# Turning an attention mask with 32x32 squares on the vector engine, in place of transposing DMAs

## The chip, the core and the metric

The kernel runs on one core of one Trainium2 chip. A core has a matrix engine (PE, with a weight-load track PEld), a vector engine (DVE), an activation engine (ACT), a general engine (POOL), and a queue engine (SP) that here only issues DMAs. The engines run their own instruction streams in order and wait for one another by semaphores. The time is device microseconds (us) of one execution.

## The reference, cut to what matters

Two graph-attention layers run over 16 batches of 1024 tokens with 256 features. `x` is float32, `adj` is an int32 matrix of zeros and ones, one per batch, and the same `adj` masks both layers.

```
for layer in (0, 1):                      # 4 heads of 64, then 8 heads of 32
    h = relu(layernorm(x))
    q, k, v = h @ Wq, h @ Wk, h @ Wv      # per head
    s = q @ k.T / sqrt(D)                 # 1024 x 1024 per head and batch
    s = where(adj > 0, s, -inf)           # row: the token that asks; column: the key
    x = x + softmax(s) @ v @ Wo + bo
```

## The kernel before, in words

**Tiling.** Everything is float32 except the mask. The scores are computed transposed: a PE matmul (L450) leaves 128 keys on the partitions and 512 asking tokens (a "half", `qh`) along the row, in a PSUM pair `ps` of 2 x 512. The DVE (L473, `exponentials`) combines a pair with the mask and writes it to SBUF as `p`; ACT (L479) takes the exponential in place; PE (L491, `weigh`) multiplies by the values into `po`. The sums of the exponentials come from POOL, which adds `p` tiles (L604), from accumulating DMAs `p<-p` (L588), and from a matmul with ones (`pz`, L343). They travel through `spread` (`sums`), `invert` (L383, then a DMA to `vd`) and `fetch` (DMAs to `inv`), and POOL scales the output `cat` with them (L402). `end_half` multiplies by Wo (L432) and adds to `x` (L437).

**Steps.** The work is a list of steps written out by hand. A step is a tile of scores: in layer 0 two key tiles of two heads, in layer 1 one key tile of four heads. The list runs layer 0 of batch 0, then for each batch `b` the 16 steps of layer 0 of batch `b+1` and the 32 steps of layer 1 of batch `b`. In the lists of due times `a` is the index of the first of these layer-0 steps, `c = a + 16` that of the first layer-1 step. I write c+7 for the layer-1 step with that index. PE issues the scores of a step two steps (LEAD) ahead of its `weigh`. There are three `ps` pairs, and every other PSUM product (`pq`, `pv`, `py`, `ph`) takes one of the same three. Layer-0 steps are run two at a time.

**Other work** (`Stream.later`) is hung on steps by number. Within a step or pair of steps the dues run after the step's own exponentials, in order of their step, and the PE-heavy ones (turn, k, q, values, end_half) run last of all. The order on every engine is thus fixed by these numbers. Layer-0 exponentials of two steps are added up by `add_tiles`: the DVE does L500 and L503, POOL the rest (L503 to L506).

**The mask** (`class Mask`, eight tiles of 128 asking tokens per batch) takes three steps. `load` (L148): a POOL DMA reads 128 rows of `adj`, 1024 int32 each, and casts to bf16. `flip` (L154): a transposing DMA from SP turns the 128 x 1024 tile so that the keys lie on the partitions. `put` (L163): ACT writes it as fp8 numbers of plus or minus 8192 into `mask[128, 8 key tiles, 512 tokens]`. The DVE reads 512 neighbouring fp8 numbers of one key tile in L473. For layer 1 `second` (L171) turns the same marks into 0 and 16384 in place. The pool `adjp` holds one `adj` and one `adjT` tile.

**Order of tokens.** `quarters` places `x` so that partition 32g+p, tile t, holds token 512 half + 128 g + 32 t + p.

**Statistics.** `norms(inp, half, i1, i2, i3, i4)` hangs the layer norm on four steps: statistics of tiles 0 and 1 on i1, of tiles 2 and 3 on i2 with the last small DVE operations (L195, L197) and POOL's power (L199, L201), then ACT's normalisation (L210) of tiles 0, 1 on i3 and of tiles 2, 3 on i4. For batch 0 layer 1 and for the first inputs `turn` then transposes on PE (L232); for the others `turn_blocks` transposes 32x32 squares on the DVE (L236) and DMAs put the squares in place (`turned`, `hT`).

Of the kernel before, what the change touches and what calls it, by code (L numbers as in the profile page):

```python
# [88 lines left out]
def fast_program(ctx, tc, a, w, loads, chk):  # L89
# [7 lines left out]
    QH = N // 512  # L97

    xp = ctx.enter_context(tc.tile_pool(name="xp", bufs=3))
    adjp = ctx.enter_context(tc.tile_pool(name="adjp", bufs=1))  # L100
    actp = ctx.enter_context(tc.tile_pool(name="actp", bufs=2))
    work = ctx.enter_context(tc.tile_pool(name="work", bufs=2))
    pp = ctx.enter_context(tc.tile_pool(name="pp", bufs=2))
# [14 lines left out]

    def quarters(of, b, half):

        rows = of[b, ts(half, 512), :].rearrange("(g t p) e -> g p t e", g=4, p=32)
        return [rows[g] for g in range(4)]

    def by_tile(cols):
# [13 lines left out]

    class Mask:
        def __init__(self, b):  # L140
            self.b, self.src, self.flipped, self.m = b, {}, {}, {}

        def load(self, t, at=None):

            if at is None:
                at = adjp.tile([P, N], BF16, tag="adj", name=f"adj_{self.b}_{t}")
            self.src[t] = at
            nc.gpsimd.dma_start(at, adj[self.b, ts(t, P), :])  # L148

        def flip(self, t, to=None):  # L150
            if to is None:
                to = adjp.tile([P, NT, P], BF16, tag="adjT", name=f"adjT_{self.b}_{t}")
            self.flipped[t] = to
            nc.sync.dma_start_transpose(to, self.src.pop(t))  # L154

        def put(self, t):

            qh = t // 4
            if t % 4 == 0:
                self.m[qh] = actp.tile(  # L160
                    [P, NT, 512], F8, tag="mask", bufs=5, name=f"mask_{self.b}_{qh}"
                )
            nc.scalar.activation(  # L163
                self.m[qh][:, :, ts(t % 4, P)], self.flipped.pop(t), AF.Identity,
                bias=w.below, scale=2.0 * EDGE, saturate=False,
            )

        def second(self, u):

            m = self.m[u // 4][:, ts(u % 4, 2), :]  # L170
            nc.scalar.activation(m, m, AF.Abs, bias=w.above, saturate=False)  # L171


# [138 lines left out]
    class Group:  # L312
# [46 lines left out]
        def spread(self):  # L359

            s = work.tile([P, 512], F32, tag="inv", name=f"s_{self.n}")
            nc.scalar.copy(tiled(s), by_tile(self.s))
            inp, k = self.inp, 2 * self.qh + self.g if self.layer else self.qh
            if k == 0:

                pool, tag = small, f"sums{self.layer}"
                if self.layer and inp.b == B - 1:
                    pool, tag = adjp, "adj"
                inp.sums = pool.tile(
                    [P, (4 if self.layer else 2) * self.n_f], F32, tag=tag, bufs=1,  # L370
                    name=f"sums_{inp.n}",
                )
            self.sn = inp.sums[:, ts(k, self.n_f)]
            for r in range(4):
                nc.sync.dma_start(
                    self.sn[ts(r, 32), :],
                    s[32 * r : 32 * r + 1, :].rearrange("r (c f) -> r c f", f=self.n_f),
                )
# [78 lines left out]
    def exponentials(st, between):  # L457


        gr = st.gr  # L460
        odd = st.j % 2
        if odd:
            st.p = None
            st.halves = [
                pp.tile([P, 2, 512], F32, tag=f"p1{i}", bufs=2, name=f"p_{st.n}_{i}") for i in range(2)
            ]
        else:
            st.p = pp.tile([P, 4, 512], F32, tag="p0", bufs=7, name=f"p_{st.n}")
            st.halves = [st.p[:, ts(i, 2), :] for i in range(2)]
        for i in range(2):  # L470
            half = st.halves[i]
            kt = st.blocks[2 * i][1]
            nc.vector.scalar_tensor_tensor(  # L473
                out=half,
                in0=gr.mask.m[gr.qh][:, kt, :].unsqueeze(1).to_broadcast([P, 2, 512]),
                scalar=-EDGE if gr.layer else BIG, in1=st.ps[i],
                op0=ALU.add if gr.layer else ALU.mult, op1=ALU.min,
            )
            nc.scalar.activation(half, half, AF.Exp, scale=gr.scale)  # L479
            if i == 0:  # L480
                for f in between:
                    f()
# [34 lines left out]
    class Stream:  # L517
# [12 lines left out]
        def later(self, i, f, *args):  # L530
            self.due.setdefault(i, []).append((f, args))
# [132 lines left out]
    def open_w(n):  # L664
# [7 lines left out]
    open_x(0, 0)  # L672


    stage = [pp.tile([P, 4, N], BF16, tag="p0", bufs=7, name=f"adj_0{i}") for i in range(2)]
    stage_t = [
        pp.tile([P, 2, NT, P], BF16, tag=f"p1{i}", bufs=2, name=f"adjT_0{i}") for i in range(2)
    ]

    def load(u):  # L680
        masks[0].load(u, stage[u // 4][:, u % 4, :])

    open_w(3)
    open_x(0, 1)
# [6 lines left out]
    load(3)  # L691
    inp.turn(0)

    def flip(u):
        to = stage[0][:, u % 4, :].rearrange("p (t q) -> p t q", q=P)
        masks[0].flip(u, stage_t[u // 2][:, u % 2, :, :] if u < 4 else to)

    flip(0)
    flip(1)
    open_w(1)  # L700
    inp.k(0)
    inp.norm(1, whole=True)
# [1 line left out]
        load(u)  # L704
    inp.q(0)
    inp.turn(1)
    mask.put(0)
    mask.put(1)
    inp.values(0)
    flip(2)  # L710
    open_x(1, 0)
    flip(3)
    open_w(5)
    open_x(1, 1)
    inp.k(1)
    mask.put(2)
    mask.put(3)
    inp.q(1)
    inp.values(1)
    open_w(len(loads))  # L720
# [29 lines left out]
    def norms(inp, half, *at, whole=False, bias=None):  # L750

        for i, f in zip(at, (inp.stats, inp.stats, inp.norm, inp.norm)):
            rest = (whole,) if i in at[2:] else ()
            later(i, f, half, (0, 1) if i in (at[0], at[2]) else (2, 3), *rest)
        later(at[3] + 1 if bias is None else bias, inp.add_bias, half)
# [13 lines left out]


    for u in range(4, NT):
        later((u - 4) // 2, flip, u)
        later(u - 1, mask.put, u)
    for t in range(NT):
        i = 5 + 2 * t
        later(i - 3, masks[1].load, t)
        later(i - 2, masks[1].flip, t)
        later(i, masks[1].put, t)
    later(9, bias_of_v)
    norms(inputs[0][1], 0, 2, 3, 5, 6, whole=True)  # L780
    half_inputs(inputs[0][1], 0, 7, 8, 10, 12)
# [2 lines left out]
    for b in range(B - 1):  # L784
        mine, a, c = inputs[1][b], first[b + 1], second[b]
        if b == 0:

            norms(mine, 0, a + 5, a + 6, a + 8, a + 9, whole=True)
            half_inputs(mine, 0, a + 11, a + 12, a + 14, a + 14)
            norms(mine, 1, a + 13, a + 14, a + 15, c, whole=True)  # L790
            half_inputs(mine, 1, c + 1, c + 3, c + 6, c + 4)
        else:
            norms(mine, 0, a - 20, a - 16, a - 15, a - 13, bias=a)
            block_inputs(mine, 0, a - 10, a - 8, a - 4, a, a + 2, a + 8)
            norms(mine, 1, a - 14, a - 10, a - 8, a - 6, bias=a + 6)
            block_inputs(mine, 1, a, a + 6, a + 7, c, c + 6, c + 2)
        for i, u in zip((0, 1, 2, 3, 4, 6, 8, 10), range(NT)):
            later(a + i, masks[b].second, u)
        if b + 2 < B:
            other, mask = inputs[0][b + 2], masks[b + 2]  # L800
            later(a + 6, open_x, b + 2, 0)
            later(a + 14, open_x, b + 2, 1)
            if b == 0:
                norms(other, 0, a + 14, a + 15, c + 2, c + 3)
                block_inputs(other, 0, c + 4, c + 5, c + 6, c + 8, c + 16, c + 18)
                norms(other, 1, c + 3, c + 4, c + 6, c + 7)
                block_inputs(other, 1, c + 10, c + 12, c + 16, c + 22, c + 26, c + 30)
            else:
                norms(other, 0, a + 10, a + 12, a + 13, a + 15, bias=c + 34)
                block_inputs(other, 0, c, c + 1, c + 2, c + 8, c + 16, c + 18)  # L810
                norms(other, 1, c, c + 4, c + 5, c + 6, bias=c + 36)
                block_inputs(other, 1, c + 7, c + 8, c + 12, c + 22, c + 26, c + 30)
            for i, t in zip((9, 13, 17, 22, 33, 37, 41, 45), range(NT)):
                later(a + i - 5, mask.load, t)
                later(a + i - (3 if i in (9, 13, 17) else 4), mask.flip, t)
                later(a + i, mask.put, t)
        else:
            last, e = inputs[1][b + 1], c + 32
            norms(last, 0, c + 5, c + 6, c + 8, c + 9)
            block_inputs(last, 0, c + 10, c + 11, c + 12, c + 14, c + 16, c + 20)  # L820
            norms(last, 1, c + 13, c + 14, c + 16, c + 17)
            block_inputs(last, 1, c + 18, c + 19, c + 20, c + 24, e + 6, e + 4)
            for u in range(NT):
                later(c + 8 + 2 * u, masks[b + 1].second, u)
# [250 lines left out]
```

## Time and profile before

| what | value |
|---|---|
| median of 3 runs | 3140.39 us (3140.25 to 3142.9) |
| the profiled execution | 3145.48 us, span of the profile 3143.4 us, granted clock 0.997 |
| DMA, share of 16 engines | 30.2% for POOL's queue, 21.1% for SP's |
| ACT | 2238.0 us busy (71%) |
| transposing DMAs (L154, SP) | 128, median 1272 ns to issue, 3.1 us to landing |
| mask put (L163, ACT) | 128, median 1136 ns |
| loads of adj (L148, POOL) | 128, median 599 ns to issue, 4.0 us to landing |

The profile lists groups of instructions by source line: engine, operation, tile written and tiles read, partitions x elements, count, then busy time, mean ns of one, and how long the engine had been idle before them. A view by stretch gives the busy time of each engine between two times. A view in order of time gives start, duration, engine, line and, in brackets, the idle time of the engine before the instruction and who ended it; "x2" means two instructions merged. [...] Busy time of PE is modelled from the starts, so a PE that waits between matmuls of one line shows partly as a longer piece.

### The profile page before, as it was taken

The numbers are of one execution on the slowest core, as the hardware profiler recorded it, in microseconds if no ns is written. First come the engines' busy times: TensorE is split into PE (matmuls) and PEld (weight loads), VectorE is DVE, ScalarE is ACT, GpSimd is POOL, SyncE is SP. The second block draws the span as 40 slices with busy tenths as digits, with TensorE's granted clock in tenths as the row PEclk, the third lists the DMA queues.
The fourth block names the chain that finished last, engine by engine and source line by source line (L and its number), as shares of the span: only waits on it lengthen the run. The fifth ranks groups of instructions, "written<-read, shape, count | busy, mean of one in ns | idle before, by whom it ended". The sixth has DMA issues, their size and how long they took to land.

```text
span 3143.4 us, 45292 instructions
## 1 busy us (share of the span) xinstructions
PE 3095.4 (98%) x16662; PEld 1215.4 (39%) x16662; DVE 2456.7 (78%) x2754; ACT 2238.0 (71%) x2440; POOL 2405.0 (77%) x1358
## 2 busy tenths in 40 slices
PE   8999999999999999999999999999999999999998
PEld 3443433434334343343434334343343433434332
DVE  5678787887878878788787878878788787887776
ACT  5667667686776767768677676766767677686765
POOL 4568778687887878878687786877868788786876
PEclk9999999999999999999999999999999999999999
DMA  7226456374554745646465463745637455472421
GB/s 131 54 48 138 105 118 125 91 145 101 121 125 98 140 101 115 132 100 130 101 127 116 103 137 92 135 101 118 125 91 149 101 118 124 99 141 62 88 63 32
DMA packets 339094, 341.26 MB, mean 109 GB/s; under 512 B 187312, under 2 KB 281776, under 8 KB 321840
## 3 DMA queue, kind: packets, MB, share of 16 engines
q0 software_dynamic: 37584, 173.03, 30.2%
q1 hardware_dynamic: 301280, 165.25, 21.1%
q8 instruction: 133, 2.18, 0.3%
q14 instruction: 97, 0.79, 0.1%
HBM read 149.95 MB, written 47.96 MB: 63 GB/s over the span
## 4 chain that ended last, share of the span: by engine, by line
PE 90%; DMA 4%; DVE 2%; POOL 2%; issue 1%; ACT 1%; SPq 0%; DVEq 0%; POOLq 0%; ACTq 0%
PE ps L450 30%; PE po L491 27%; PE pq L266 13%; PE pv L302 7%; PE py L432 7%; PE pz L343 4%; DMA p<-p 4%; POOL p L604 1%; DVE p L473 1%; ACT p L479 0%; PE ph L232 0%; ACT hn L210 0%; PE py L417 0%; DVE p L503 0%; DMA hT<-turned 0%
## 5 line engine op out<-in xcount | busy, mean ns | idle before, releaser
L473 DVE SCALAR_TENSOR_TENSOR p<-mask,ps 128x1024 f32<-128x1024 fp8e5 x1536 | 1785.2, 1214 | 404.4 <-PE ps L450 399.4
L479 ACT ACTIVATE p<-p 128x1024 f32<-128x1024 f32 x1536 | 1612.7, 1056 | 657.5 <-DVE p L473 596.1
L604 POOL TENSOR_TENSOR p<-p,p 128x1024 f32<-128x1024 f32 x510 | 1214.1, 2437 | 194.1 <-PE po L491 169.9
L450 PE MATMUL ps<-qT,kT 32*128 32x512 f32 (+1 forms) x6144 | 1104.9, 628 | 6.9 <-DVE p L473 4.3
L491 PE MATMUL po<-p,v 128*32 128x512 f32 (+1 forms) x6144 | 979.8, 600 | 3.1 <-ACT cat L354 2.8
L450 PEld LDWEIGHTS ps<-qT,kT 32*128 32x128 f32 (+1 forms) x6144 | 374.5, 184 | 667.5 <-issue 300.7
L491 PEld LDWEIGHTS po<-p,v 128*32 128x32 f32 (+1 forms) x6144 | 233.3, 118 | 682.8 <-issue 465.2
L504 POOL TENSOR_TENSOR p<-p 128x1024 f32<-128x1024 f32 x128 | 301.9, 2359 | 131.9 <-DVE p L503 121.0
L503 POOL TENSOR_TENSOR p<-p,p 128x1024 f32<-128x1024 f32 x64 | 150.3, 2349 | 187.0 <-DVE p L500 115.4
L266 PE MATMUL pq<-hT,wk 128*128 128x512 f32 x512 | 239.3, 611 | 2.6 <-DMA hT<-turned 1.4
L302 PE MATMUL pv<-wv,hT 128*128 128x256 f32 x1024 | 237.8, 385 | 0.0
L266 PE MATMUL pq<-hT,wq 128*128 128x512 f32 x512 | 236.6, 605 | 0.0
L432 PE MATMUL py<-wo,cat 128*128 128x256 f32 x1008 | 234.0, 385 | 1.2 <-DVE p L473 1.2
L402 POOL TENSOR_TENSOR cat<-cat,inv 128x512 f32<-128x512 f32 x127 | 180.7, 1466 | 52.6 <-DMA inv<-vd 50.1
L302 PEld LDWEIGHTS pv<-wv,hT 128*128 128x128 f32 x1024 | 189.5, 190 | 71.4 <-DVE p L473 15.3
L432 PEld LDWEIGHTS py<-wo,cat 128*128 128x128 f32 x1008 | 186.7, 190 | 73.2 <-issue 35.1
L500 DVE TENSOR_TENSOR p<-p 128x1024 f32<-128x1024 f32 x128 | 174.6, 1364 | 0.0
L343 PE MATMUL pz<-p,ones 128*32 128x512 f32 x1248 | 163.9, 597 | 6.2 <-DMA p<-p 5.4
L219 POOL TENSOR_TENSOR x<-x,bo 128x1024 f32<-128x1024 f32 x64 | 155.5, 2476 | 17.5 <-DMA bo<-in_bo_dram 17.5
L437 DVE TENSOR_TENSOR x<-py,x 128x1024 f32<-128x1024 f32 x63 | 77.1, 1224 | 114.0 <-PE py L432 113.1
L354 ACT COPY cat<-po 128x512 f32<-128x512 f32 x128 | 73.3, 572 | 129.3 <-PE py L432 110.5
L506 POOL TENSOR_TENSOR p<-p,p 128x1024 f32<-128x1024 f32 x64 | 151.3, 2365 | 5.0
(51 smaller groups left out, 1651.0 us busy)
## 6 DMA issues: line engine op xcount, KB each, us to landing
p<-p POOLq DMA_DIRECT2D x133, 1024.0 KB, 8.0
adj<-in_adj_dram POOLq DMA_DIRECT2D x128, 256.0 KB, 4.0
turned<-hn SPq DMA_DIRECT2D x58, 512.0 KB, 3.4
hT<-turned SPq DMA_DIRECT2D x232, 128.0 KB, 3.3
x<-in_x_dram SPq DMA_DIRECT2D x128, 128.0 KB, 2.7
inv<-vd SPq DMA_DIRECT2D x128, 128.0 KB, 3.0
inv<-vd SPq DMA_DIRECT2D x252, 64.0 KB, 2.2
out_dram<-x SPq DMA_DIRECT2D x124, 128.0 KB, 2.3
```

What stands on the lines that cost most here:

```text
L266: nc.tensor.matmul(pq[:, m, :], wt[self.layer][:, c, ts(m, P)], self.hT[half][:, c, :], start=(c == 0), stop=(c == 1),)
L302: nc.tensor.matmul(pv[:, i, :], self.hT[half][:, c, ts(i, P)], w.v[self.layer][:, c, :], start=(c == 0), stop=(c == 1),)
L343: nc.tensor.matmul(self.s[ts(r, 32), :], w.ones.to_broadcast([P, 32]), of, start=start, stop=stop)
L402: nc.gpsimd.tensor_mul(o, o, inv)
L432: nc.tensor.matmul(py[:, i, :], self.half.cat[:, c, ts(i, P)], w.o[self.layer][:, c, :], start=(c == 0), stop=(c == 1),)
L450: nc.tensor.matmul(st.ps[i // 2][:, i % 2, :], gr.inp.kT[r * D : (r + 1) * D, gr.g, ts(kt, P)], gr.inp.qT[gr.qh][r * D : (r + 1) * D, gr.g ...
L473: nc.vector.scalar_tensor_tensor(out=half, in0=gr.mask.m[gr.qh][:, kt, :].unsqueeze(1).to_broadcast([P, 2, 512]), scalar=-EDGE if gr.layer ...
L479: nc.scalar.activation(half, half, AF.Exp, scale=gr.scale)
L491: nc.tensor.matmul(gr.o[r * D : (r + 1) * D, :], gr.inp.v[:, kt, h * D : (h + 1) * D], st.halves[i // 2][:, i % 2, :], start=(kt == 0), st ...
L500: nc.vector.tensor_add(a, a, b)
L504: nc.gpsimd.tensor_add(a, a, b)
L604: nc.gpsimd.tensor_add(half, half, of)
```

## The change

**Tokens.** `quarters` now places token 256 t + 128 half + 4 p + g at partition 32g+p, tile t. Asking tokens and keys change places alike, and output rows go back by the same function.

**Loads.** A load takes, for one pair (half, t), the 128 asking tokens (r, g) and spreads each row of `adj` over four partition groups k: partition 32k+r holds four tokens g with 256 neighbouring columns each. A row of 1024 int32 is thus read in four pieces of 256.

**Put.** ACT writes four neighbouring columns of one token as four fp8 marks, one 32-bit word. `put` runs one step before its former place for the second half of batch 0, and at its former place otherwise.

**Flip.** `flip` is now a DVE transpose of 4 x 2 squares of 32 x 32 words, in place, 256 words per partition, one step after `put`. After it the partition counts keys, and a word holds the marks of four keys, one in each of four key tiles. L473 therefore reads its 512 marks four bytes apart. `second` takes a quarter of the same bytes.

**Pools.** `adjp` holds two `adj` tiles and no `adjT`; the staging tiles `stage_t` of batch 0 are gone.

**Statistics.** For batch 0, layer 1, those of half 0 move from a+5, a+6 to a+6, a+7; of half 1 from a+13, a+14 to a+14, a+15, and the normalisation of half 1 from a+15, c to c, c+1. The DVE's order shows what comes of it: before, the statistics of tiles 0 and 1 stood ahead of the addition to `x` (L437) of the same half; now they stand behind it.

The order of PE's instructions is the same in both kernels. SP has 128 instructions fewer, the DVE 128 more.

```diff
     def quarters(of, b, half):
-        rows = of[b, ts(half, 512), :].rearrange("(g t p) e -> g p t e", g=4, p=32)
+        rows = of[b].rearrange("(t h p g) e -> h g p t e", h=QH, p=32, g=4)[half]
...
-        def load(self, t, at=None):
-                at = adjp.tile([P, N], BF16, tag="adj", name=f"adj_{self.b}_{t}")
-            nc.gpsimd.dma_start(at, adj[self.b, ts(t, P), :])
-        def flip(self, t, to=None):
-            nc.sync.dma_start_transpose(to, self.src.pop(t))
+        def load(self, u, at=None):
+                at = adjp.tile([P, 4, 256], BF16, tag="adj", name=f"adj_{self.b}_{u}")
+            rows = adj[self.b].rearrange("(t h r g) (k c) -> h t k r g c", h=QH, r=32, g=4, k=4)
+            nc.gpsimd.dma_start(at, rows[u // 4, u % 4])
+        def squares(self, u):
+            m = self.m[u // 4].rearrange("p h q t -> p (h q t)").bitcast(F32)
+            return m.rearrange("p (h g t q) -> p t g h q", h=2, g=4, q=32)[:, u % 4]
...
-                    [P, NT, 512], F8, tag="mask", bufs=5, name=f"mask_{self.b}_{qh}"
+                    [P, 2, 512, 4], F8, tag="mask", bufs=5, name=f"mask_{self.b}_{qh}"
+            to = self.m[qh].rearrange("p h (g t q) k -> p t g h (q k)", g=4, q=32)[:, u % 4]
...
+        def flip(self, u):
+            nc.vector.transpose(self.squares(u), self.squares(u))
...
-                in0=gr.mask.m[gr.qh][:, kt, :].unsqueeze(1).to_broadcast([P, 2, 512]),
+                in0=gr.mask.m[gr.qh][:, kt // 4, :, kt % 4].unsqueeze(1).to_broadcast([P, 2, 512]),
...
     for u in range(4, NT):
-        later((u - 4) // 2, flip, u)
-        later(u - 1, mask.put, u)
+        later(u - 2, mask.put, u)
+        later(u - 1, mask.flip, u)
...
-        later(i - 2, masks[1].flip, t)
         later(i, masks[1].put, t)
+        later(i + 1, masks[1].flip, t)
...
-            norms(mine, 0, a + 5, a + 6, a + 8, a + 9, whole=True)
+            norms(mine, 0, a + 6, a + 7, a + 8, a + 9, whole=True)
-            norms(mine, 1, a + 13, a + 14, a + 15, c, whole=True)
+            norms(mine, 1, a + 14, a + 15, c, c + 1, whole=True)
...
             for i, t in zip((9, 13, 17, 22, 33, 37, 41, 45), range(NT)):
                 later(a + i - 5, mask.load, t)
-                later(a + i - (3 if i in (9, 13, 17) else 4), mask.flip, t)
                 later(a + i, mask.put, t)
+                later(a + i + 1, mask.flip, t)
```

## The prediction on record

> **What bounds the kernel now.** I read the busy time of each engine first, then PE by stretch.
>
> ```profile
> PE 3095.4 (98%) x16662; PEld 1215.4 (39%) x16662; DVE 2456.7 (78%) x2754; ACT 2238.0 (71%) x2440; POOL 2405.0 (77%) x1358
> ...
> 901.40:977.80 76.40, 76.40 (x342) 31.44 (x338) 59.51 (x64) 52.07 (x56) 55.19 (x30) 1.00 0.48 98
> 977.80:1093.60 115.80, 115.47 (x698) 43.58 (x696) 96.04 (x108) 87.19 (x98) 96.50 (x56) 1.00 0.60 127
> ```
>
> The last two lines are one batch in the middle (columns: length, then PE, PEld, DVE, ACT, POOL busy, clock, DMA share, GB/s): 76.4 us of layer 0, in which PE has no gap, and 115.8 us of layer 1 with 0.33 us of gap. DVE is idle 16.9 and 19.8 us, POOL 21.2 and 19.3. PE is the bound in the whole middle. What it still loses hides in longer pieces, in order of time (start, length):
>
> ```profile
> 1066.79 1.14 PE L450 MATMUL ps<-qT,kT 32*128 32x512 f32 x8
> 1067.86 1.06 PE L491 MATMUL po<-p,v 128*32 128x512 f32 x8
> 1068.86 1.51 PE L450 MATMUL ps<-qT,kT 32*128 32x512 f32 x8
> ...
> 991.87 2.09 PE L450 MATMUL ps<-qT,kT 32*128 32x512 f32 x8
> ```
>
> A step's eight `ps` matmuls take 1.14 unhindered; 1.51 is a wait of 0.37 for a `ps` pair that the DVE has not read yet, four or five such per batch; 2.09 at step c+3 is a wait of 0.95. With 0.3 before one `pz` (for DMA p<-p) and small change this is about 5 us per batch of 192. So a change off PE can win little, and loses only where it lengthens these waits or makes new ones.
>
> **Part by part.** Sums are made on the span, 3143.4; the execution was 3145.5, 5.1 above the median of 3140.4, and I carry differences over to the median.
>
> ```profile
> L473 DVE SCALAR_TENSOR_TENSOR p<-mask,ps 128x1024 f32<-128x1024 fp8e5 x1536 | 1785.2, 1214 | 404.4 <-PE ps L450 399.4
> ...
> L437 DVE TENSOR_TENSOR x<-py,x 128x1024 f32<-128x1024 f32 x63 | 77.1, 1224 | 114.0 <-PE py L432 113.1
> ...
> L236 DVE STREAM_TRANSPOSE hn<-hn 128x1024 f32<-128x1024 f32 x58 | 71.7, 1237 | 1.9 <-ACT hn L210 1.9
> ...
> L148 POOL DMA_DIRECT2D adj<-in_adj_dram x128 | 83.7, 656 | 12.8 <-DMA adjT<-adj 11.2 <-issue 1.1
> ```
>
> *Flips added.* L236 turns 1024 words in 1.237. DVE additions of 1024 and 256 words (L437 1.224, L732 0.42) give 1.04 ns a word, so 256 words need 1.237 - 768 x 0.00104 = 0.44, and 0.36 of the DVE's time, since consecutive DVE rows overlap by 0.08. 128 x 0.36 = 46 us in all, 2.9 a batch: two flips in layer 0, six in layer 1 (after c+2, c+7, c+18, c+22, c+26, c+30). Behind each stands the next L473 pair, and PE waits for that. The DVE's idle time after these places in the middle batch is 0.27, 1.71 (one step on), 1.20, 0.38 (one step on), 1.28 and 2.44: only the first does not cover 0.36. Path: 0.1 a batch, 1.4 us in 14 batches. Without that cover it is 2.9 a batch, 41 us. Each flip waits for `put` on ACT one step before: at c+1 `put` ends at 989.85, and the DVE comes to the flip at 992.8; I add no wait.
>
> [...]
>
> *L473 reads marks four bytes apart.* No row shows that. The nearest is L437, one SBUF float beside PSUM, thus also four bytes a step: 1.224 against 1.214, 0 on the path. The dear end is L500, two SBUF floats beside a busy POOL, mean 1.364: +0.15.
>
> *Put, second:* same element counts; L163 1.136 and L171 stay. 0. *`quarters`:* pieces of 1 KB before and after; 0.
>
> *Loads.* A load goes from 128 pieces to 512. POOL issues one in 0.6 now; SP issues 128 pieces (turned) in 0.438 and 256 (hT) in 0.622, 1.44 ns a piece, which would make 0.6 + 384 x 0.00144 = 1.15. The ends are 0.6 and, if all grows with the pieces, 2.4. I take 1.15. POOL's idle time before its next waiting work is 2.3, 2.4, 3.7 in layer 0, and 1.65, 2.0, 0.5, 1.0, 1.3 in layer 1; the 0.5 is followed by 3.1 of slack. So +0.55 costs 0. At +1.8 the load at 1057.8 makes the L604 two pairs on 0.7 late, whose `p` buffer the DVE wants 0.1 later: 0.7 a batch, 10 us.
>
> *Transposing DMAs removed.* 128 x 1.27 us of SP's time, and SP's waits in front of them, 605 us, which hold up what is queued behind. What is late next: at most places nothing, since ACT waited 1.5 us in all for `adjT`. One place matters:
>
> ```profile
> 977.39 1.28 SPq L154 DMA_TRANSPOSE adjT<-adj  x1
> 978.72 0.60 SPq L385 DMA_DIRECT2D vd<-vn  x1
> 980.90 2.41 SPq L394 DMA_DIRECT2D inv<-vd  x4
> ...
> 985.94 3.49 POOL L402 TENSOR_TENSOR cat<-cat,inv 128x512 f32<-128x512 f32 x2 [3.31 <-DMA inv<-vd]
> ...
> 986.01 2.30 DVE L500 TENSOR_TENSOR p<-p 128x1024 f32<-128x1024 f32 x1
> 988.41 2.11 DVE L503 TENSOR_TENSOR p<-p,p 128x1024 f32<-128x1024 f32 x1
> ```
>
> `vd` stands behind a transposing DMA. Without it `inv` lands 1.3 sooner, and POOL's two L402 start at 984.6. Now they run beside L500 and L503, which take 2.30 and 2.11 where 1.22 is usual; the late DVE is what costs PE 0.95 at 991.87. Between 0 and 0.95 a batch can go; L402, 2.8 long for two where undisturbed (1016.67), then still overlaps L500, so I take 0.3: 14 x 0.3 = -4.2. [...]
>
> *Start.* PE runs nearly unbroken from 14 to 38.5 on the layer norm and projections; put and flip of the first half sit in idle ACT and DVE time there. From 48.9 on DVE is late: flips 4 to 7 and one of batch 1 add 5 x 0.36 = 1.8 to it. But `hn` of batch 1, for which PE waits at 66.94, comes 0.5 sooner, as one `put` (1.14) has left ACT's queue in front of it, and the DVE afterwards idles 2.25. Net -0.5 (ends -1.5 and +1.8).
>
> *Batch 0's statistics.* Two pairs of statistics (4 operations, 1.2 us) leave places where the DVE then idled 2.44 and 5.6, for places where it is late. At 160.43 L473 comes at least 1.2 later, more if L195 has to wait behind POOL, as at 204.18 (1.20 in place of 0.16); PE waits there already (`ps` x16 at 166.34). I take 2. And normalising half 1 now comes at c+1, right in front of PE's `turn` of the same step, which started at 213.69; ACT can have `hn` only at about 216.4. I take 2.5, the later wait of 0.9 for hT included. +4.5 (ends 0 and 9).
>
> *Tail:* the last 200 us have no load, put or flip: 0.
>
> **Sum:** 1.4 - 4.2 - 0.5 + 4.5 = +1.2. Span 3144.6, median 3141.6: no change. (0.2%, 6.3 us, is about what a measurement of this kernel tells from none.)
>
> **Rivals.**
> - *A, freed queues win more, faster.* For it: 0.95 and the `pz` wait of 0.3 recur each batch. All of the first: 14 x 0.95 = 13.3, less 0.5, plus 4.5 and 0: 3131. Both at full, statistics 2: 3124. Against: `pz` waits for p<-p beside hT<-turned, and no transposing DMA is near.
> - *B, POOL's issue grows with the pieces, slower.* It decides from about 1.7 us an issue; at 2.4, as above, 10 more: 3152.
> - *C, the strided read of L473 meets POOL, slower.* At 1.364, a step needs 0.30 more of the DVE; each of the four or five waits of 0.37 spans two steps: 5 x 0.6 = 3 a batch, 42: 3184. Flips without cover give the same place, 41. Against it: L437 runs 1.223 to 1.226 in 63 cases.
> - *D, batch 0's statistics at their dear end*, +9: 3146 to 3150.
> - *E, it does nothing that shows:* all covered, batch 0 too: 3140.
>
> **Chances.** Forecast 0.44 and E 0.02: same 0.46. A 0.18: faster. B 0.15, C 0.14, D 0.07: slower 0.36. The range leaves out C and A's far end: 3129 to 3156, in which the forecast's own is 3135 to 3146.
>
> **What would show it.** Flips of 0.44 (over 0.6 is against me); L473 within 1.21 to 1.23; adj issues near 1.15 on POOL (over 1.7 speaks for B); L500 at c+1 shorter and the `ps` at c+3 nearer 1.8; the waits of 0.37 unchanged in number; between 150 and 225 us PE 4 to 5 us later than now against the first step; SP without L154. I am wrong if PE's pieces in the middle lengthen, or if `put` to flip makes the DVE wait.

## The result and the profile after

The changed kernel took 3187.0 us (median of 4 runs, 3184.4 to 3189.5) beside 3140.9 before: a ratio of 1.0146, 95% interval 1.0128 to 1.0163. It is slower by 46 us, where I had forecast no change. In the two profiled executions the spans differ by 39.3 us (3182.7 against 3143.4). The rest lies in which executions were profiled: the one before was 4.6 us above the median of 3140.9, the one after 2.6 below its own. All that follows explains the 39.3. The line numbers of load and put are one higher after, those from `second` on four (L473 is now L477, L450 is L454).

First, from the page of the kernel before, the Pool queue (packets, MB and share) and two DMA issues (POOLq and SPq name the engine that issues; the last number is us to landing), then from its list of waits that of the DVE for `x` (total, times, longest):

```profile
q0 software_dynamic: 37584, 173.03, 30.2%
...
adj<-in_adj_dram POOLq DMA_DIRECT2D x128, 256.0 KB, 4.0
...
out_dram<-x SPq DMA_DIRECT2D x124, 128.0 KB, 2.3
```

```profile
DVE st L191 <- DMA x<-in_x_dram: 6.7, 2, 4.2
```

From the page of the changed kernel (engines; then the Pool queue; then a group and DMA issues):

```profile
PE 3119.6 (98%) x16662; PEld 1221.8 (38%) x16662; DVE 2521.7 (79%) x2882; ACT 2236.4 (70%) x2440; POOL 2540.5 (80%) x1358
...
q0 software_dynamic: 283344, 173.82, 33.8%
...
L149 POOL DMA_DIRECT2D adj<-in_adj_dram x128 | 207.6, 1622 | 4.6 <-issue 4.0
...
adj<-in_adj_dram POOLq DMA_DIRECT2D x128, 256.0 KB, 9.7
...
out_dram<-x SPq DMA_DIRECT2D x124, 128.0 KB, 2.8
```

A load of the mask now takes 1.62 us to issue (0.66 before) and 9.7 to land (4.0 before). It had 144 packets; it has 2064, since 283344 less 133 x 144 for `p<-p` is 128 x 2064. Only 512 of them are pieces of 512 bytes; the trace's own records give the other 1552 as 4 bytes each. I call these empty, since the 512 pieces are the whole 256 KB of the load.

The groups of the DVE that the forecast spoke of, changed kernel:

```profile
L477 DVE SCALAR_TENSOR_TENSOR p<-mask,ps 128x1024 f32<-128x1024 fp8e5 x1536 | 1786.2, 1214 | 373.8 <-PE ps L454 360.0 <-POOL p L608 6.7 <-POOL p L507 4.0
...
L195 DVE BATCH_NORM_STATS2 st<-x 128x6 f32<-128x256 f32 x256 | 107.5, 420 | 42.0 <-DMA x<-in_x_dram 37.5
...
L170 DVE STREAM_TRANSPOSE mask<-mask 128x256 f32<-128x256 f32 x128 | 55.1, 431 | 11.4 <-ACT mask L164 11.4
```

The strided read and the flips cost what I had said (1214 ns, 431 ns). What is new is the line between: the DVE waits 37.5 us for `x` in front of statistics (6.7 before, where the line is L191).

Where is the time lost? PE runs the same 16662 instructions in the same order in both kernels, so the n-th can be set beside the n-th. I call the difference of their starts the lag. It is -1.8 us at 140 us, +6.2 at 230 (batch 0's statistics lie between), 6.3 at 400, 16.3 at 1000, 39.0 at 2850 and 39.4 at 3100. So 8.0 come from batch 0's statistics, 32.8 from 13 batches behind it, 2.5 each (1.6 to 3.0; the 14th, which the prediction counted too, loses nothing), and the tail adds 0.4. Within a batch nearly all of it falls on the first nine steps of layer 1. In order of time there, first the store and the next `x` in the kernel before, then the changed kernel (the batch shown in the prediction; start, length):

```profile
971.93 1.79 SPq L440 DMA_DIRECT2D out_dram<-x  x4
...
975.54 1.75 SPq L135 DMA_DIRECT2D x<-in_x_dram  x4
```

```profile
983.29 1.63 POOL L149 DMA_DIRECT2D adj<-in_adj_dram  x1 [0.21 <-issue]
...
986.08 2.32 SPq L444 DMA_DIRECT2D out_dram<-x  x4
...
994.47 1.75 SPq L135 DMA_DIRECT2D x<-in_x_dram  x4
...
999.94 0.43 DVE L195 BATCH_NORM_STATS2 st<-x 128x6 f32<-128x256 f32 x1 [3.31 <-DMA x<-in_x_dram]
...
1001.30 2.26 PE L454 MATMUL ps<-qT,kT 32*128 32x512 f32 x8
1003.56 3.72 PE L306 MATMUL pv<-wv,hT 128*128 128x256 f32 x16
1003.73 4.26 POOL L406 TENSOR_TENSOR cat<-cat,inv 128x512 f32<-128x512 f32 x2 [6.60 <-DMA inv<-vd]
```

The third load of the batch is issued 2.8 us ahead of the output's store. The next `x` goes into the buffer that this store empties, so SP holds it back: it starts 8.4 us after the store (3.6 before: 975.54 less 971.93). Of the 132 `out_dram` stores, 48 take over 6 us to land, up to 7.1; in the kernel before, e1, e5, e7 and e9 (below) none does. Behind the `x` on SP stand `vd`, `inv`, `turned` and `hT`. The DVE comes to the statistics 3.31 us before `x` is there, and the next two L477 stand behind them in its queue; `ps` at 1001.30 takes 2.26 where 1.14 is usual.

The theory (F, for few engines) is an inference from counts. A load's source has the four blocks of 256 columns as its outermost dimension, and I take its pieces to go through 4 of the 16 DMA engines and the empty packets to the other 12. In the kernel before a load has 128 pieces and 16 packets of 4 bytes; 12 x 128 + 16 = 1552 and 4 x 128 = 512 fit the counts after. The trace doesn't name the engine of a packet, so the four are not shown: besides the counts only the number of pieces that run at once (e1) speaks for them. By the theory, whatever else needs those four engines before the load has landed (9.7 us) is late. Rivals: I, POOL's longer issue; V, the flips on the DVE.

### The profile page after: what moved, and what is told of

Same layout as the page of the kernel before. It is cut to its first block, busy times and chain, and to the rows that moved or that the text cites. A ratio compares the mean times of both kernels' runs of the same rounds, so it can differ in the third digit from the quotient of the medians.

```text
span 3182.7 us, 45121 instructions
## 1 busy us (share of the span) xinstructions
PE 3119.6 (98%) x16662; PEld 1221.8 (38%) x16662; DVE 2521.7 (79%) x2882; ACT 2236.4 (70%) x2440; POOL 2540.5 (80%) x1358
## 3 DMA queue, kind: packets, MB, share of 16 engines
q0 software_dynamic: 283344, 173.82, 33.8%
q8 instruction: 133, 2.18, 0.3%
## 4 chain that ended last, share of the span: by engine, by line
PE 79%; DMA 8%; DVE 7%; issue 2%; SPq 1%; POOL 1%; ACT 1%; DVEq 0%; POOLq 0%; ACTq 0%
PE ps L454 27%; PE po L495 23%; PE pq L270 11%; PE py L436 7%; PE pv L306 6%; PE pz L347 4%; DMA p<-p 4%; DVE p L477 3%; DMA out_dram<-x 3%; DMA x<-in_x_dram 1%; POOL p L608 1%; DVE p L507 1%; DVE st L195 1%; DVE p L504 1%; SPq L444 1%
## 5 line engine op out<-in xcount | busy, mean ns | idle before, releaser
L477 DVE SCALAR_TENSOR_TENSOR p<-mask,ps 128x1024 f32<-128x1024 fp8e5 x1536 | 1786.2, 1214 | 373.8 <-PE ps L454 360.0
L608 POOL TENSOR_TENSOR p<-p,p 128x1024 f32<-128x1024 f32 x510 | 1217.8, 2449 | 135.9 <-PE po L495 115.8
L454 PE MATMUL ps<-qT,kT 32*128 32x512 f32 (+1 forms) x6144 | 1125.3, 628 | 19.7 <-DVE p L477 15.9
L454 PEld LDWEIGHTS ps<-qT,kT 32*128 32x128 f32 (+1 forms) x6144 | 380.8, 184 | 694.9 <-issue 288.8
L507 POOL TENSOR_TENSOR p<-p,p 128x1024 f32<-128x1024 f32 x64 | 150.7, 2355 | 200.1 <-DVE p L504 120.3
L406 POOL TENSOR_TENSOR cat<-cat,inv 128x512 f32<-128x512 f32 x127 | 193.0, 1566 | 91.9 <-DMA inv<-vd 89.8
L149 POOL DMA_DIRECT2D adj<-in_adj_dram x128 | 207.6, 1622 | 4.6 <-issue 4.0
L592 POOL DMA_DIRECT2D p<-p x133 | 121.8, 916 | 53.1 <-POOL p L608 19.5
```

Source lines behind the costliest of these rows:

```text
L149: nc.gpsimd.dma_start(at, rows[u // 4, u % 4])
L454: nc.tensor.matmul(st.ps[i // 2][:, i % 2, :], gr.inp.kT[r * D : (r + 1) * D, gr.g, ts(kt, P)], gr.inp.qT[gr.qh][r * D : (r + 1) * D, gr.g ...
L477: nc.vector.scalar_tensor_tensor(out=half, in0=gr.mask.m[gr.qh][:, kt // 4, :, kt % 4].unsqueeze(1).to_broadcast([P, 2, 512]), scalar=-EDG ...
L608: nc.gpsimd.tensor_add(half, half, of)
```

## The experiments

Ratios are against the kernel before, with 95% intervals; lags as above, from each kernel's profiled execution.

| kernel | median us | ratio | lag at 140 | 230 | 2850 |
|---|---|---|---|---|---|
| changed | 3187.0 | 1.0146 (1.0128 to 1.0163) | -1.8 | 6.2 | 39.0 |
| e1 rows outermost | 3171.8 | 1.0093 (1.0076 to 1.0110) | -2.1 | 7.5 | 21.1 |
| e2 before, with blocks outermost | 3387.7 | 1.0784 (1.0766 to 1.0802) | 22.9 | 24.6 | 234.5 |
| e3 no flip | 3186.0 | 1.0139 (1.0122 to 1.0156) | -3.0 | 6.0 | 41.7 |
| e4 old statistics | 3178.0 | 1.0113 (1.0097 to 1.0130) | -1.5 | -1.2 | 32.4 |
| e5 four DMAs a load | 3151.7 | 1.0026 (1.0015 to 1.0036) | -1.9 | 7.0 | 7.8 |
| e6 e5 and old statistics | 3146.8 | 1.0010 (1.0000 to 1.0020) | -1.4 | -1.4 | -1.7 |
| e7 third load two steps earlier | 3147.6 | 1.0014 (1.0005 to 1.0024) | -2.4 | 7.3 | 2.6 |
| e8 before, POOL held 1.03 longer | 3144.0 | 1.0004 (0.9994 to 1.0013) | -0.7 | 1.0 | -0.9 |
| e9 e7 and old statistics | 3138.7 | 0.9989 (0.9980 to 0.9998) | -2.4 | -0.5 | -4.7 |
| e10 statistics behind the late x | 3166.9 | 1.0081 (1.0067 to 1.0094) | -2.2 | 7.5 | 20.3 |
| e11 e9 with three flips | 3209.7 | 1.0217 (1.0203 to 1.0231) | 5.1 | 6.5 | 63.7 |
| e12 e9 without flips | 3138.0 | 0.9985 (0.9976 to 0.9994) | -2.5 | -2.5 | -7.6 |

**e1, the same pieces, another outermost dimension.**

```diff
-            rows = adj[self.b].rearrange("(t h r g) (k c) -> h t k r g c", h=QH, r=32, g=4, k=4)
+            rows = adj[self.b].rearrange("(h g p) (k c) -> h k p g c", h=QH, p=P, k=4)
```

> The changed kernel, but each load reads its 512 pieces (still 256 columns each) in another order: partition p takes four rows 128 apart and one block of columns, so that the outermost dimension of the source counts 128 and no longer 4. The mask is then not the reference's; the rest is untouched. Theory F (the loads use 4 of the 16 DMA engines, for some 9 us each, and hold up SP's transfers): load packets on all engines, landing 4 to 5 us in place of 9.7, out_dram back to 2.3, the time back to 3146 to 3158. Theory I (POOL's issue, 1.62 in place of 0.65, is the cause): the issue stays near 1.6, since there are still 512 pieces, and so does the time, 3182 to 3190. Theory V (the flips on DVE): 3182 to 3190.

Of the packets, 528 a load now, 512 are pieces, and a load lands in 4.0. DMA share in 40 slices (tenths) and GB/s around one load, first the changed kernel (961 to 975 us), then e1 (1067 to 1073):

```profile
DMA  9400003687677995333333533310000000000000
GB/s 284 48 0 0 0 0 10 31 94 60 74 40 84 169 259 125 51 48 61 56 60 66 116 48 50 41 19 0 0 0 0 0 0 0 0 0 0 0 0 0
...
q0 software_dynamic: 2064, 0.27, 20.0%
```

```profile
DMA  0000000000046799999999731000000000000000
GB/s 0 0 0 0 0 0 0 0 0 0 0 51 79 82 164 177 188 188 188 205 195 145 92 39 12 0 0 0 0 0 0 0 0 0 0 0 0 0 0 0
...
q0 software_dynamic: 528, 0.26, 33.6%
```

In the changed kernel a burst of empty packets (and the end of `inv`) is followed by some 3.5 us at mostly three tenths of the engines and 41 to 66 GB/s; in e1 the same bytes run at nine tenths and 190. Counted from the records, e1 moves up to 340 such pieces in one us and the changed kernel 53 to 97, about a quarter. A piece itself takes 64 ns in both (mean), but in the changed kernel never more than 8 run at once (the 114 loads after 100 us), in e1 up to 31. That fits theory F's first half; on which engines they ran stays an inference. The time fell only by 15 us, though, and stayed 14 above what theory F had expected, and the kernel is no test against I: the issue fell too, to 0.87 (I had expected 1.6). The 14 us that the middle still loses (lag 7.5 to 21.1) belong to a stall the changed kernel does not have: the first nine steps of layer 1, where the changed kernel lost, gain 5.6 us over the 13 batches, and the last 41 us of layer 1 lose 19.0. The group of e1:

```profile
L214 ACT ACTIVATE hn<-x,shift,rstd 128x256 f32<-128x256 f32 x256 | 138.2, 588 | 42.4 <-DMA turned<-hn 31.6
```

In the batch shown, `turned` starts 0.55 us behind a 1 MB `p<-p` and lands in 10.9 us, where 3.5 is the median. ACT waits 3.9 for the `hn` buffer, `put` stands behind it, and the flip stops the DVE for 4.1. The two in e1, then at the same place of the changed kernel, in order of time:

```profile
1072.99 0.87 POOL L592 DMA_DIRECT2D p<-p  x1 [0.30 <-POOL p L608]
...
1073.54 0.32 SPq L245 DMA_DIRECT2D turned<-hn  x1
```

```profile
1081.50 0.33 SPq L245 DMA_DIRECT2D turned<-hn  x1
...
1081.74 0.86 POOL L592 DMA_DIRECT2D p<-p  x1 [0.30 <-POOL p L608]
```

So in the changed kernel `turned` goes first, and lands in 4.1. The same holds in the other batches: in e1 it starts 0.54 to 0.88 us behind that `p<-p` and lands in 5.8 to 10.9; in the changed kernel, e5, e7 and e9 it starts 0.2 to 0.8 ahead (once in each of the changed kernel, e7 and e9 0.1 behind) and lands in 2.8 to 5.9. The stall thus goes with the order of the two, which some tenths of a us decide. No run changed that order alone.

**e2, the same pattern in the kernel before.**

```diff
-            nc.gpsimd.dma_start(at, adj[self.b, ts(t, P), :])
+            rows = adj[self.b, ts(t, P), :].rearrange("(r g) (k c) -> k r g c", g=4, k=4)
+            nc.gpsimd.dma_start(at.rearrange("p (g c) -> p g c", c=256), rows)
```

> The kernel before, with its transposing DMAs and without flips, but each load takes the pieces of the changed kernel (four blocks of 256 columns outermost, 512 pieces). The mask is then not the reference's. Theory F: landing near 10 us, out_dram from 2.3 to some 2.8 in the median and over 5 at the layer change; +25 to +45, 3165 to 3186, and more if the transposing DMAs behind the loads come late. Theory I: issue of 1.6, and about the same +25 to +45. Theory V: no change, 3141.

It lost 245 us, by a mechanism of its own: there is one `adj` buffer, the transposing DMA waits for the slow load, and POOL stands 157 us in front of the next load, its additions queued behind. So it gives no price for F or I. It shows that the load's pattern does harm without any flip, which theory V had not expected, and two signs of F: a load lands in 9.6, and `out_dram` in 2.7 (2.3 before).

**e3, no flips.**

```diff
-            nc.vector.transpose(self.squares(u), self.squares(u))
+            pass
```

> The changed kernel without the 128 flips: the mask stays unturned, so its values are not the reference's, everything else is done. Theory V: 41 us and more come back, 3140 to 3148. Theories F and I: only the few places where the DVE is late gain 0.36 each, 1 to 8 us; 3179 to 3186.

1 us came back, within the resolution. Theory V falls, as the price of the flips in this kernel; e12 asks again without the late loads.

**e4, batch 0's statistics as before.**

```diff
-            norms(mine, 0, a + 6, a + 7, a + 8, a + 9, whole=True)
+            norms(mine, 0, a + 5, a + 6, a + 8, a + 9, whole=True)
...
-            norms(mine, 1, a + 14, a + 15, c, c + 1, whole=True)
+            norms(mine, 1, a + 13, a + 14, a + 15, c, whole=True)
```

> The changed kernel with batch 0's statistics at the steps where the kernel before has them. My step on these statistics (4.5, ends 0 and 9), together with the 7.8 us by which PE falls behind between 150 and 225 us: 5 to 9 us come back, 3178 to 3182. If that fall is the loads' doing, as theory F could also have it: under 2 us, 3185 to 3187.

9.0 us came back, the dear end; the lag at 230 goes from 6.2 to -1.2. The changed kernel in order of time, where that lag arises:

```profile
208.79 0.16 DVE L199 TENSOR_TENSOR ve<-mv,numbers 128x4 f32<-128x4 f32 x1 [2.12 <-POOL rstd L203]
...
209.17 1.40 DVE L282 TENSOR_SCALAR qT<-pq,bq 128x512 f32<-128x512 f32 x2
```

Three places: at 162 PE loses 2.3 and regains 0.6; at 219 `turn` waits 2.15 for `hn`. The third is the one above: two statistics now follow each other closely, the second may write the single `ve` buffer only after POOL has read it for the first, and `qT`, for which PE waits 2.14, stands behind it, 3.8 later than before (205.38).

**e5 and e6, the reference's mask by four DMAs for each load.** Each takes one block of columns, so that 32 tokens are outermost.

```diff
-            nc.gpsimd.dma_start(at, rows[u // 4, u % 4])
+            for k in range(4):
+                nc.gpsimd.dma_start(at[ts(k, 32)], rows[u // 4, u % 4][k])
```

> The changed kernel, but each load is issued as four DMAs, one for each block of 256 columns, so that the outermost dimension of the source is 32 tokens and no longer 4 blocks. The result is the reference's. The pieces, their number and their size stay. Theory F (four DMA engines): the packets of 4 bytes fall from 1552 a load to 64, out_dram lands in 2.3, the DVE no longer waits some 2.5 us a batch for x; POOL's issue grows to 4 x 0.6 = 2.4 or so. The time falls to 3150 to 3165. Theory I (POOL's issue): 2.4 in place of 1.62 makes it slower than the changed kernel, 3195 to 3220.

> The four-DMA loads of the run above together with batch 0's statistics at their former steps, which alone gave back 9 us. The result is the reference's. Theory F: both gains add up, 3141 to 3156. Theory I: 3186 to 3211.

e5: the loss in the middle is gone (lag 7.0 at 230, 7.8 at 2850), though POOL now spends 288 us on these issues (0.55 each in the median, 2.25 a load) in place of 208. This separates F from I: more issue, 35 us less time. e6 adds the statistics: 5 us in the median (9 alone), 8.4 in the lag at 230 (7.4 alone).

**e7, one load of eight moved.**

```diff
-                later(a + i - 5, mask.load, t)
+                later(a + i - (7 if i == 17 else 5), mask.load, t)
```

> The changed kernel with one load of eight moved: the third of each batch two steps earlier, from a+12 to a+10, so that it has landed before the out_dram and x transfers at the layer change begin. The result is the reference's. Theory F with the place that I read (out_dram, x, statistics, the DVE's order): the DVE's wait for x goes, 1.5 to 2.3 us a batch come back in 14 batches, 3155 to 3167. If the loads cost by POOL's issue or anywhere else: 3183 to 3190.

It gave back more than I expected, 39 us: the middle now gains (7.3 to 2.6). The loads still issue in 1.62 and land in 9.6; the other seven, as slow as ever, cost next to nothing. The waits of the DVE for `x`, changed kernel, then e7 (total, times, longest):

```profile
DVE st L195 <- DMA x<-in_x_dram: 37.5, 15, 4.3
```

```profile
DVE st L195 <- DMA x<-in_x_dram: 7.3, 2, 4.3
```

**e8, POOL held up in the kernel before.**

```diff
             nc.gpsimd.dma_start(at, adj[self.b, ts(t, P), :])
+            spare = small.tile([P, 4], F32, bufs=1, tag="spare", name=f"spare_{self.b}_{t}")
+            nc.gpsimd.tensor_tensor(spare, w.eps, w.mhalf, ALU.pow)
```

> The kernel before, with one POOL power of 128x4 (1.03 us, a row of the trace; its result is not used) behind each load: POOL is held up as long as by the new issue (0.97 longer), while the load itself stays whole and fast. The result is the reference's. Theory I: most of the 33 us that the middle lost, 3165 to 3180. Theory F: 0 to 8, 3141 to 3150.

1.0004, no difference that can be measured. Theory I falls a second time.

**e9, both repairs** (the edits of e4 and e7).

> The changed kernel with the two repairs that worked alone: the third load two steps earlier, and batch 0's statistics at their former steps. The result is the reference's. If these two are the whole loss, 3147.6 - 9 = 3138 to 3140, a little under the kernel before (my -4.2 in the middle, and the start, would then show). If they overlap: 3142 to 3147.

As the first case had it: 3138.7, ratio 0.9989. It is the only version with the flips that is ahead of the kernel before, by 3 us (0.6 to 6).

**e10, the statistics behind the late x, loads untouched.**

```diff
-                norms(other, 1, c, c + 4, c + 5, c + 6, bias=c + 36)
+                norms(other, 1, c + 3, c + 4, c + 5, c + 6, bias=c + 36)
```

> The changed kernel with one item moved: the statistics of tiles 0 and 1 of the next batch's second half go from step c to c+3, behind the late x, so that the DVE doesn't wait for x with its pairs of scores queued behind. The loads stay as they are. The result is the reference's. If the chain load, out_dram, x, DVE carries the loss: the waits at c+1 and before pv go (1.2 + 0.8 a batch in 13 batches), 3158 to 3170. If the late x is only a companion, and the late inv or something else carries it: 3182 to 3189.

20 us came back. So the queue position of these statistics on the DVE carries about 0.6 of the 33 us. What is left, 1.0 a batch (lag 7.5 to 20.3), shows, in the batch looked at above, at the first `pz` of layer 1 (+1.4), which waits for POOL's L510, and at L199, which takes 3.41 us beside POOL's L608 (+1.0), with 0.9 gained before them: L406 still waits 6.8 for `inv`, so POOL is late.

**e11 and e12, the price of a flip without late loads.**

```diff
-            nc.vector.transpose(self.squares(u), self.squares(u))
+            for _ in range(3):
+                nc.vector.transpose(self.squares(u), self.squares(u))
```

> The kernel with both repairs, with each flip done three times in place of once (the result is the same): 2 x 128 x 0.36 = 92 us more for the DVE. It asks how much cover the flips have once the loads are out of the way. By my terms for the flips, one place in eight without cover: two more flips there cost 0.7 to 1 a batch, and the places with 0.4 to 1.3 of idle time begin to cost too: 10 to 40 us over the run with both repairs, 3149 to 3180. Fully covered: under 5.

e12 takes the line out of e9 as e3 did.

> The kernel with both repairs (3138.7) without its 128 flips, so that the mask stays unturned and its values are not the reference's; the rest is done. It prices the flips where no late load hides them. My term, one uncovered place in eight: 1.4 us come back, 3136 to 3139. No cover: 41 us, 3098.

Without its flips e9 gains 0.7 in the median and 3 us of lag: 46 us of DVE time cost 1 to 3. Two more flips a load, 92 us, cost 71, far over my 10 to 40. Part of that is again the stall of e1: ACT waits 33.3 us for `turned`, 14 times, and the flips 44.7 for `put`; 43 of the 68 us of lag over e9 fall on the last 41 us of layer 1, where that stall lies. So this run is no clean price.

## Why the prediction was wrong, point by point

The forecast was 3141.6 with a range to 3156. Against the terms of its sum, in lag:

| step | predicted | measured |
|---|---|---|
| start | -0.5 (-1.5 to 1.8) | -1.8, 0.3 beyond its end |
| batch 0's statistics | 4.5 (0 to 9) | 8.0 (e4 gave back 7.4, and 9.0 in the median) |
| middle: flips, loads, freed transposes | 1.4 + 0 - 4.2 = -2.8 | 32.8 |
| tail | 0 | 0.4 |

- **The step that failed is "Loads".** I priced a load as time on POOL and as pieces, and wrote that +0.55 costs 0. The issue came out at 1.62, between my ends, and that really costs nothing: e7 keeps it and gains 4.7 over the middle, and e8, which holds POOL as long, can't be told from the kernel before. The term of 0 was worth some 37 us all the same, the 32.8 lost in the middle and the 4.7 that e7 gains. I never asked how many of a load's pieces run at once, how long it takes from the first piece to the last, and which transfers of SP start in that time. Where I did look at SP's queue at the layer change, I saw only what the missing transposing DMA would bring forward. The diff showed the outermost 4. In the changed kernel 512 of a load's 2064 packets carry data, and never more than 8 of these ran at once (the 114 loads after 100 us), where e1, with 128 outermost, has up to 31. From e1 to the changed kernel the time from the first piece to the last went from 2.0 to 6.8 (medians), the landing from 4.0 to 9.7; in e5, with 32 outermost, each quarter of a load lands in 2.6. That four engines carry the pieces is still my inference.
- **Rival C named the nearest time, 3184, for a reason that is false.** L477 stayed at 1214 ns, and the flips are covered (e3, e12). Rival B's condition, an issue above 1.7, was nearly met, and would have cost little even so: e5, at 2.25 a load, stands 5.5 us of lag behind e7 over the middle, from whatever cause. Rival D is right as a term, not in its total: nearly its dear end happened, at three places instead of two; the single `ve` buffer I had not seen.
- **Flips: right.** 0.431 for 0.44, and 1 to 3 us on the path for 1.4. e9, which has the flips, is ahead of the kernel with the transposing DMAs (0.9989). Of the 11.4 us that flips wait for `put`, 9.1 are at the start; in the middle it is 0.2 a batch.
- **`quarters`, put, second, the strided read: right**, each at nothing: `out_dram` lands in 2.3 again when the load is out of its way (e7, e9).
- **Transposing DMAs removed: about right in size, hidden by the load.** With both repairs the lag falls by 4.2 over the middle (-0.5 to -4.7), flips included, where I had -2.8; without the flips (e12) by 5.1, where I had -4.2. No run takes the transposing DMAs out alone. My signs for it were half wrong. In e7 at step c+1, in order of time:

```profile
992.97 2.27 DVE L504 TENSOR_TENSOR p<-p 128x1024 f32<-128x1024 f32 x1
995.35 1.23 DVE L507 TENSOR_TENSOR p<-p,p 128x1024 f32<-128x1024 f32 x1
```

The first addition still takes 2.27 (2.30 before) and the second falls from 2.11 to 1.23. I had said that the first would get shorter. Over the 13 batches the second takes 2.1 in twelve before, in three in e7 and in four in e9; the first falls less, in the mean from 1.9 to 1.7 and 1.6. In the batch shown, the second L406 of e7 (992.89 to 994.16) runs beside the first addition only and the first L406 (990.91 to 992.19) beside neither; the two L402 of the kernel before (985.94 to 989.43) run beside both.

## What to carry to other kernels

When an edit changes a DMA's access pattern, read its outermost dimension before counting its pieces, and look at packets, landing time and DMA share beside its issue time: here the same 512 pieces landed in 9.7 us with 4 outermost and in 4.0 with 128 (e1). The slow loads did harm almost only where a short, awaited transfer ran beside them: moving one load of eight by two steps was worth 39 us, and spreading all of them 35. When an engine's busy time grows and the kernel gets slower, test the cover (e3, e12) before believing that this growth is the cause.

## What the runs showed of the hardware beyond that

- A load with 4 outermost has, beside its 512 pieces, 1552 packets of 4 bytes, of 8 ns each (mean). Its issue takes POOL 1.62 us, against 0.87 for the same 512 pieces in 528 packets (e1) and 0.66 for 128 pieces in 144 (the kernel before).
- A store of 512 KB (`turned`) that starts 0.54 to 1.05 us behind a 1 MB accumulating DMA (`p<-p`) landed in 5.8 to 10.9 us in the middle batches of e1 and e11, 28 stores, and in 2.8 to 5.9 where it started 0.2 to 0.8 ahead of it (changed kernel, e5, e7, e9). The kernel before lies at the edge: 0.43 to 0.68 behind, landing in 2.6 to 9.9, over 7 in three of 14. What decides there was not found.
- A small DVE operation with two SBUF inputs (L199, 128x4) took 2.18 us in the changed kernel and 3.41 in e10 beside POOL's L608, and ended with it, where 0.16 is usual.
